# Descending rows of pairs, nodes' ends beside later pairs, and half-size checks in a four-layer graph kernel

## The chip, the cores and the metric

The kernel runs on one core of one Trainium2 chip. The time is the device time of one execution in microseconds; lower is better. Engines are called PE (TensorE), DVE (VectorE), ACT (ScalarE), POOL (GpSimd) and SP (SyncE, which issues most DMAs). PEld is PE's loading of weights.

## The reference

Four graph layers over 4096 nodes of 64 features with one dense 0/1 adjacency of 4096 x 4096. Each layer is fed the normalised, rectified x and added to it:

```python
h = relu(layernorm(x)); x = x + L0(h, adj)   # multi-head graph attention
h = relu(layernorm(x)); x = x + L1(h, adj)   # hyperbolic attention over pairs
h = relu(layernorm(x)); x = x + L2(h, adj)   # neighbours' mean
h = relu(layernorm(x)); x = x + L3(h, adj)   # last 100 neighbours, decayed by rank
```

The layers in question are the last three, cut to what is computed:

```python
# L1
att = sigmoid(left[:, None] + right[None, :] + b) * adj
support = einsum('ij,ijd->id', att, logmap(x[:, None], x[None], c))  # log of a distance
out = proj(expmap(x, support, c), c)      # norms, a tanh, roots: per node
# L2
deg = clip(adj.sum(1) + 1, 1); z = concat([X, (adj @ X + X) / deg], 1) @ W + b
out = relu(z) / max(norm(relu(z)), 1e-12)
# L3
rank = cumsum(adj != 0, 1); deg = rank[:, -1:]; k = minimum(deg, 100)
w = (adj != 0) * where(rank - (deg - k) > 0, 0.5 ** (deg - rank), 0)
out = w @ (X @ weight) + bias
```

## The kernel before, in words

There are 128 partitions, 32 blocks of 128 nodes, 8 groups of 4 blocks (512 nodes) and 4 quarters of 8 blocks. The time up to 1190 us of the span is layer 0 and preparation, which the change leaves alone.

**Layer 1, pairs** (`pairs_fast`, L2253). The 8 x 8 pairs of groups are symmetric in distance, so the list of jobs (L2270) holds 36: rows gi ascending from 0, and in each the columns gj from 0 to gi. A job reads two edge tiles nm (one on the diagonal), makes scores with PE and a sigmoid on ACT (`score_pair`, L2290), a distance with PE, a sigmoid and a Square on ACT (`distance` L2312, `square` L2327), multiplies on DVE (`factor` L2334, `weigh` L2341), transposes the factor on PE and multiplies again for the other direction (`turn`, L2348: the transposes L2353, the multiply L2356), and sums in fp32 on PE (`sums` and `last_column` through `add_up`, L2363). Sums over gj go to the bank acci, kept through a row; sums over gi to accj, which `bring` (L2403) adds into VT (128 x 4096) after each job. The diagonal job ends a row, and its acci is copied to VT first.

**The written order.** Inside `in_order()` every instruction of DVE, ACT and PE is chained to the one written before it on its engine. The pairs' loop (L2422) is a software pipeline with four slots s = 0 to 3 for each job: in one turn it finishes job n - 1, sums job n, weighs n + 1 and measures n + 2. POOL and SP are not chained. Outside `in_order()` a scheduler orders the instructions by readiness and by their place in the program.

**Checks.** The fast layers need an adjacency of zeros and ones. `check_rows` (L958, its instruction L960) reads raw tiles of the adjacency on DVE and adds up what is not 0 or 1 into a column of `bad`. There are 64 tiles of 128 x 2048 (1 MB, loaded by SP, two buffers); the pairs' loop takes most of them, one or two a job, and layer 3 takes the rest by halves of 128 x 1024 (32 instructions) in 2 of 3 iterations from the 16th on (L2936).

**Layer 1, nodes' ends** (`finish_steps` L2452, then `norm_steps` L972, then `nodes` L2602). A generator for each quarter: 8 transposing matmuls pvt out of VT (L2471), the multiply that leaves PSUM (L2475), about 40 DVE operations of 128 x 512 or 128 x 8, Square on ACT (L2491), two roots and a tanh on ACT (L2500, L2520, L2503), the layernorm with its own Square and root (L985, L991), and the split of h in two half-precision parts HH (L2605, L2608, L2612). HH lies in the memory of XA_all, which the distances of the pairs read (XC, XH). A generator yields after each step, True where the next waits for another engine. After all pairs, and in a written order, a loop (L2615 on) runs the four quarters one after the other, with up to 7 steps of the next one put into the waits (two at a wait).

**Layer 2.** The degree and neighbour sums of nodes 0 to 2047 come first: HH against all edges, 8 steps of q ascending, four banks nacc (L2754) and one dc (L2764), from a PSUM pool of six banks (L2744). Then `layer2_group` (L2674) runs for pairs of groups (`in_turn`, L2731, alternates two generators): pz (L2680, L2683), norm, residual, layernorm, transposes tr (L1008), psup (L2717), the split into SS. Nodes 2048 to 4095 come as four `segment`s (L2792: nacc L2802, dc L2811), which also fill a plate of edge counts, plate1 (L2824), from which `rank_rows` (L2739) makes the ranks that layer 3 adds to. There are four pairs of groups in all, called 1 to 4.

**Layer 3** (loop L2924, in a written order). 64 iterations: `ranks` (pv: L2860, L2868), `clamp` (L2877, on ACT L2882 and DVE L2884), `add_up` (sacc, L2892), `bring` (L2906) for the output. Its PSUM pools ps_sacc (2 banks) and ps_v (4 banks), L2846, are opened after layer 2's six have been closed; the pool `misc` of two banks serves both.

Of the kernel before, what the change touches and what calls it, by code (L numbers as in the profile page):

```python
# [25 lines left out]
P = 128  # L26
# [29 lines left out]
F_C = 1186.920286584489  # L56

HW = N // 2
NS = HW // G
HB = NB // 2  # L60
# [776 lines left out]
def kernel(  # L837
# [76 lines left out]
    bad = npool.tile([P, 2 * NB + 2 + NB // 2], F32, name="bad")  # L914
# [37 lines left out]
    def load_rows(pool, c):  # L952

        raw = pool.tile([P, HW], F32, name="raw", tag="raw", bufs=2)
        nc.sync.dma_start(raw, adjT[c % NB * P : (c % NB + 1) * P, c // NB * HW : (c // NB + 1) * HW])
        return raw

    def check_rows(raw, at):  # L958

        nc.vector.scalar_tensor_tensor(  # L960
            raw, raw, 0.0, raw, ALU.is_gt, ALU.not_equal, accum_out=bad[:, at : at + 1]
        )

    def count_odd(pool, c):
        check_rows(load_rows(pool, c), c)

    todo = iter(range(2 * NB))
# [4 lines left out]
    def norm_steps(bs, wide, tag, act=True):  # L972
# [18 lines left out]
        nc.scalar.activation(var, var, AF.Sqrt, bias=eps_t, scale=1.0 / D)  # L991
        yield True
        nc.vector.reciprocal(var, var)
# [55 lines left out]
    with ExitStack() as l0:  # L1049
# [259 lines left out]
        with ExitStack() as pa:  # L1309
# [49 lines left out]
            with in_order():  # L1359
# [87 lines left out]
                nc.vector.tensor_reduce(bad[:, 2 * NB : 2 * NB + 1], tn[:, 0:HS], AX.X, ALU.max)  # L1447
# [488 lines left out]
        with ExitStack() as ob:  # L1936
# [47 lines left out]
            with in_order():  # L1984
# [79 lines left out]
                nc.vector.tensor_scalar(bad[:, 2 * NB + 1 : 2 * NB + 2], sp, SPREAD, None, ALU.is_gt)  # L2064
# [188 lines left out]
    def pairs_fast(es, VT):  # L2253
# [16 lines left out]
        jobs = [(gi, gj) for gi in range(NG) for gj in range(gi + 1)]  # L2270
        edges, sig, far, accs, squares = {}, {}, {}, {}, {}

        with ExitStack() as ss:
# [129 lines left out]
            def bring(gi, gj):  # L2403
                if gi == gj:
                    acci = accs.pop(gi)
                    nc.vector.tensor_copy(VT[0:D, grp(gi)], acci[D : 2 * D])
                    nc.vector.tensor_copy(VT[D : 2 * D, grp(gi)], acci[0:D])
                nc.vector.tensor_tensor(VT[:, grp(gj)], VT[:, grp(gj)], accs.pop("j"), ALU.add)
                del far[gi, gj]
                for way in ways(gi, gj):  # L2410
                    del sig[way], edges[way]

            def check_edges():
                c = next(todo, None)
                if c is not None:
                    count_odd(work, c)
# [5 lines left out]
            with in_order():  # L2422
                for n in range(-2, len(jobs) + 1):
# [3 lines left out]
                    for s in range(4):  # L2427
# [11 lines left out]
                        if later:  # L2439
                            distance(*later, s)  # L2440
                            if s % 2:
                                square(*later, s - 1)
                        if s == 1 and soon:
                            factor(*soon)
                        if n >= 0 and (s == 2 or s == 0 and (not now or now[0] == now[1])):
                            check_edges()
                        if s == 3 and soon:
                            weigh(*soon)
                            for _ in range(2 if n < 0 else 0):
                                check_edges()  # L2450

    def finish_steps(bs, VQ, VT, fold_v, pabs, f, f2, kp, pf, ac2, wide, ps):  # L2452
# [14 lines left out]
        for g in range(bs.start // GB, bs.stop // GB):  # L2467
            pt = ps.tile([P, GB, D1], F32, name="pvt", tag="misc")
# [31 lines left out]
        nc.scalar.activation(un, un, AF.Sqrt)  # L2500
        yield True
        nc.vector.tensor_tensor(arg, un, kp[:, bs], ALU.mult)
        nc.scalar.activation(arg, arg, AF.Tanh)  # L2503
        nc.vector.reciprocal(un, un)
# [7 lines left out]
        nc.vector.tensor_scalar(one2, xu, p2c, 1.0, ALU.mult, ALU.add)  # L2512
        nc.vector.tensor_tensor(den, ac2[:, bs], uu, ALU.mult)
# [6 lines left out]
        nc.scalar.activation(pp, pp, AF.Sqrt)  # L2520
# [5 lines left out]
        nc.vector.reciprocal(pp, pp)  # L2526
# [12 lines left out]
        yield from norm_steps(bs, wide, "fat")  # L2539
# [5 lines left out]
    def layers_fast(es, wide, *sums):  # L2545
        HO2 = N // 4
        NK = HO2 // G
        cp = es.enter_context(tc.tile_pool(name="lconst", bufs=1))
# [21 lines left out]
        for i, unit in enumerate((1.0 / VALH, 1.0 / (LO * VALH))):  # L2570
# [11 lines left out]
        HH, SS = (  # L2582
            t.rearrange("p (b s d) -> p b s d", s=2, d=D)
            for t in (XA_all.bitcast(F16)[:, 0:N], XA_all.bitcast(F16)[:, N:])
        )
# [10 lines left out]
        ready = []  # L2596

        QB = NB // 4  # L2600

        def nodes(bs):  # L2602
            yield from finish_steps(bs, *sums, wide, ps)
            hs = wide.tile([P, QB, D], F32, name="hs", tag="fat")
            nc.scalar.activation(HH[:, bs, 0, :], h[:, bs], AF.Copy, scale=VALH)  # L2605
            yield True
            ready.append(
                nc.vector.scalar_tensor_tensor(  # L2608
                    hs, h[:, bs], VALH, HH[:, bs, 0, :], ALU.mult, ALU.subtract
                )  # L2610
            )
            nc.scalar.activation(HH[:, bs, 1, :], hs, AF.Copy, scale=LO)  # L2612


        quarters = [nodes(slice(b, b + QB)) for b in range(0, NB, QB)]  # L2615
        with in_order():
            for quarter, after in zip(quarters, quarters[1:] + [iter(())]):
                most = 7
                for wait in quarter:
                    for _ in range(min(2, most) if wait else 0):  # L2620
# [41 lines left out]

# [380 lines left out]
```

## Time and profile before

| what | us |
|---|---|
| median of 3 runs (lowest, highest) | 1974.12 (1970.68, 1974.84) |
| the profiled execution's own time | 1974.73 |
| its span on the core | 1973.0 |
| mean granted PE clock | 0.943 |
| busy PE / PEld / DVE | 1773.5 / 827.7 / 1596.4 |
| busy ACT / POOL | 1424.0 / 89.3 |
| pairs of layer 1, from and to | 1190 to 1644 |
| the four writes of HH (a quarter each) | 1675.95, 1692.97, 1710.0, 1726.93 |
| first pz of the four pairs of groups | 1743.3, 1759.9, 1779.5, 1808.2 |
| first pv of layer 3; PE's last work | 1812.4; 1965 |

The times of a profile come from one execution. In its rows L is the line of the kernel; a group shows what it writes, an arrow and what it reads, by the names of the program (the names are those of the first tile in a memory: `XAf` stands for HH, `who` for the value that L2475 makes, `LDf` for blk). "x" is the number of instructions. Brackets at the end give the idle time before and what ended it. Start times are from the start of the span. A busy PE is not PE at its peak, and PEclk is the clock that it was granted as a share of the full one.

### The profile page before, as it was taken

What the parts mean: (1) busy time and instruction counts of PE and PEld (TensorE: products, weight loads), DVE (VectorE), ACT (ScalarE), POOL (GpSimd) and SP (SyncE); (2) the same over time, 40 slices, a digit from 0 to 9 for tenths busy, and PEclk for the clock granted to TensorE, in tenths of its full rate; (3) what the DMA queues carried; (4) which work ended last, traced back from release to release, by engine and by line L of the source; (5) the groups of instructions that cost most, each with busy time, mean ns of one, the idle gap of its engine ahead of it and who ended that gap; (6) DMA issues with size and microseconds to landing.
All of it is one profiled execution on the core that took longest, in us unless ns stands there. A gap on an engine that the chain in (4) does not pass through costs nothing. (4 is left out here: it accounts for less than half of the span.)

```text
span 1973.0 us, 44405 instructions
## 1 busy us (share of the span) xinstructions
PE 1773.5 (90%) x19367; PEld 827.7 (42%) x19367; DVE 1596.4 (81%) x2378; ACT 1424.0 (72%) x1461; POOL 89.3 (5%) x127
## 2 busy tenths in 40 slices
PE   5889999999999989998599968999999994899998
PEld 3444444454444445444244442233333332355433
DVE  5769998998779988997768867888887878755676
ACT  2769888899778887995579956777777772333565
POOL 2000100100000000000111100000000001000000
PEclk8889999999999999998699976999999996898999
DMA  8946665325211111102255515543443435342584
GB/s 112 178 127 103 103 102 71 143 107 199 114 50 50 50 50 55 56 2 76 87 182 182 191 34 193 171 144 118 150 144 122 139 103 194 129 128 88 165 276 158
DMA packets 136698, 239.06 MB, mean 121 GB/s; under 512 B 15607, under 2 KB 104999, under 8 KB 122759
## 3 DMA queue, kind: packets, MB, share of 16 engines
q1 hardware_dynamic: 121964, 194.00, 29.4%
q0 software_dynamic: 14528, 42.13, 12.3%
q8 instruction: 153, 2.51, 0.5%
q14 instruction: 53, 0.43, 0.1%
HBM read 245.37 MB, written 49.46 MB: 149 GB/s over the span
## 5 line engine op out<-in xcount | busy, mean ns | idle before, releaser
L1213 ACT ACTIVATE st<-srow,nt 128x2048 int8<-128x2048 f32 x352 | 682.9, 1994 | 90.3 <-DVE B L1219 89.0
L1219 DVE TENSOR_TENSOR B<-st,mres 128x1024 int32<-128x1024 int32 x256 | 311.6, 1220 | 65.1 <-PE accC L1549 39.4
L1549 PE MATMUL accB<-B,ybh 128*32 128x512 fp8e4 x3072 | 256.6, 383 | 18.7 <-DVE B L1219 18.5
L1549 PEld LDWEIGHTS <-ybh 128*32 128x32 bf16 (+1 forms) x6656 | 179.1, 97 | 210.9 <-issue 56.4
L1549 PE MATMUL accC<-B,ycn 128*32 128x512 fp8e4 x2272 | 227.8, 380 | 1.2 <-issue 1.2
L1549 PE MATMUL accC<-mres,ych 128*32 128x512 fp8e4 x2272 | 228.1, 381 | 0.0
L1549 PE MATMUL accD<-B,ybh 128*32 128x512 fp8e4 x2048 | 207.6, 384 | 2.1 <-DVE h L1681 2.1
L1207 DVE TENSOR_SCALAR st<-srow,nt 128x2048 uint8<-128x2048 f32 x160 | 205.3, 1284 | 1.8
L2363 PE MATMUL accj<-sg,who 128*64 128x512 f32 (+1 forms) x512 | 196.7, 614 | 6.4 <-DVE sg L2356 5.9
L2363 PE MATMUL acci<-sg,who 128*64 128x512 f32 (+1 forms) x512 | 196.7, 614 | 0.0
L2319 ACT ACTIVATE yt<-pu,consts 128x512 f32<-128x512 f32 x144 | 98.6, 686 | 97.9 <-PE pu L2318 97.8
L2308 ACT ACTIVATE sg<-pl,rb 128x512 f32<-128x512 f32 x256 | 160.7, 678 | 7.8 <-PE pl L2303 4.7
L1549 PEld LDWEIGHTS <-ych 128*32 128x32 f16 x4096 | 117.6, 97 | 115.3 <-issue 10.2
L1549 PE MATMUL accL<-B,ybh 128*32 128x512 fp8e4 x1536 | 158.0, 387 | 3.6 <-DVE h L1680 3.6
L960 DVE SCALAR_TENSOR_TENSOR raw<-raw 128x2048 f32<-128x2048 f32 (+1 forms) x80 | 148.4, 1856 | 3.3 <-DMA raw<-in_adj_dram 3.3
L1213 ACT ACTIVATE st<-srowo,nto 128x1024 int8<-128x1024 f32 x128 | 138.1, 1138 | 16.3 <-DVE B L1219 13.9
L1227 DVE TENSOR_TENSOR C<-B,mres 128x1024 int32<-128x1024 int32 x114 | 139.5, 1224 | 3.1
L1549 PE MATMUL accC<-C,ych 128*32 128x512 fp8e4 x1824 | 124.0, 383 | 5.3 <-DVE C L1227 5.2
L2882 ACT ACTIVATE w3b<-pv 128x512 int16<-128x512 f32 x160 | 85.3, 596 | 52.9 <-issue 34.3
L2356 DVE SCALAR_TENSOR_TENSOR sg<-pf,sg 128x512 f32<-128x512 f32 x112 | 72.1, 685 | 38.7 <-PE pf L2353 38.7
L2297 PE MATMUL pl<-nm,noid 128*128 128x512 fp8e4 x256 | 82.3, 393 | 13.7 <-ACT sg L2308 13.0
L1549 PEld LDWEIGHTS <-ycn 128*32 128x32 f16 x2272 | 66.1, 98 | 62.1 <-issue 3.2
(515 smaller groups left out, 2738.8 us busy)
## 6 DMA issues: line engine op xcount, KB each, us to landing
raw<-in_adj_dram SPq DMA_DIRECT2D x64, 1024.0 KB, 5.6
mo<-edges SPq DMA_DIRECT2D x32, 512.0 KB, 4.0
noedge<-nmo POOLq DMA_DIRECT2D x32, 512.0 KB, 3.9
nm<-noedge SPq DMA_DIRECT2D x64, 256.0 KB, 3.0
m<-edges SPq DMA_DIRECT2D x32, 512.0 KB, 5.5
srow<-srow_d SPq DMA_DIRECT2D x15, 1024.0 KB, 7.8
mres<-in_adj_dram POOLq DMA_DIRECT2D x8, 1024.0 KB, 36.1
edges<-in_adj_dram POOLq DMA_DIRECT2D x8, 1024.0 KB, 15.0
```

The source lines that it names most:

```text
L960: nc.vector.scalar_tensor_tensor(raw, raw, 0.0, raw, ALU.is_gt, ALU.not_equal, accum_out=bad[:, at : at + 1])
L1207: nc.vector.tensor_scalar(st[:, i, :].bitcast(U8), srow, negs[:, i : i + 1], EDGE, ALU.is_gt, ALU.mult)
L1213: nc.scalar.activation(st[:, i, :], srow, AF.Sign, bias=negs[:, i : i + 1], scale=-1.0)
L1219: nc.vector.tensor_tensor(B.bitcast(I32), st.bitcast(I32), edges.bitcast(I32), ALU.bitwise_and)
L1227: nc.vector.tensor_tensor(C.bitcast(I32), B.bitcast(I32), edges.bitcast(I32), ALU.bitwise_xor)
L1549: ins = nc.tensor.matmul(acc[k * O : (k + 1) * O, :], lhsT=values, rhs=moving(k), start=start, stop=stop,)
L2297: nc.tensor.matmul(pl, lhsT=noid, rhs=nm[:, b, :].bitcast(F8), start=True, stop=False)
L2308: nc.scalar.activation(sg[:, b0 + k, :], pl, AF.Sigmoid, bias=rb[:, j : j + 1], scale=1.0)
L2319: nc.scalar.activation(far[gi, gj][:, b, :], pu, AF.Sigmoid, bias=nb_t, scale=2.0 * DIST_K / (DIST_S * DIST_S),)
L2356: nc.vector.scalar_tensor_tensor(v[:, t, :], pf, F_K3, v[:, t, :], ALU.add, ALU.mult)
L2363: nc.tensor.matmul(acc[r : r + n, :], lhsT=XQ[:, src, cols], rhs=w, start=start, stop=stop)
L2882: nc.scalar.activation(wk, pvs[i, k], AF.Relu)
```

## The change

1. Jobs go by descending rows, (7, 0) first and (0, 0) last. Row 7 copies accj into VT, all later ones add; the diagonal's halves of acci are added.
2. After the diagonal of rows 6, 4 and 2, the quarter made of groups gi and gi + 1 is complete, and the part of XA under its HH is no longer read. Its `nodes` generator then runs in the pairs' loop, one step a slot (two at s = 2; the first two, which use a bank of ps_f for pvt, only at odd s). The quarter of row 2 is held before its first root. After the pairs the rest of it and the quarter of groups 0 and 1 run as before, with up to 12 steps, three at a wait.
3. In steps beside pairs the three roots are an estimate made on DVE from the bits of the number and three Newton steps on POOL (12 instructions).
4. Checks are 128 halves of 128 x 1024 (512 KB) with four loads asked ahead. In the order that was built, 60 stand in the pairs (none while a quarter's end is under way), 28 from there to the end of layer 2 (7 of them among the last ends of quarters) and 40 in layer 3's last 40 iterations.
5. Layers 2 and 3 share ps_sacc (2 banks) and ps_v (4). Layer 2's first sums take the edges by descending q, and the transposes of h descend too. plate1 and its rank_rows stand in iteration 16 of layer 3.

```diff
-        jobs = [(gi, gj) for gi in range(NG) for gj in range(gi + 1)]
+        jobs = [(gi, gj) for gi in reversed(range(NG)) for gj in range(gi + 1)]
+        ends, held, beside = [], [], [True]
...
             def bring(gi, gj):
+                accj = accs.pop("j")
+                if gi == NG - 1:
+                    nc.vector.tensor_copy(VT[:, grp(gj)], accj)
+                else:
+                    nc.vector.tensor_tensor(VT[:, grp(gj)], VT[:, grp(gj)], accj, ALU.add)
                 if gi == gj:
                     acci = accs.pop(gi)
-                    nc.vector.tensor_copy(VT[0:D, grp(gi)], acci[D : 2 * D])
-                    nc.vector.tensor_copy(VT[D : 2 * D, grp(gi)], acci[0:D])
-                nc.vector.tensor_tensor(VT[:, grp(gj)], VT[:, grp(gj)], accs.pop("j"), ALU.add)
+                    for to, r in ((0, D), (D, 0)):
+                        half = VT[to : to + D, grp(gi)]
+                        nc.vector.tensor_tensor(half, half, acci[r : r + D], ALU.add)
+                    if gi % 2 == 0 and gi:
+                        bank = lambda: ps_f.tile([P, G], F32, name="pf", tag="pf")
+                        ends.append([nodes(gi * GB, bank, beside), 0, *(["last"] if gi == 2 else [])])
...
+            def check_edges(n):
+                for _ in range(n):
+                    if len(todo) + len(ahead) > CHECKS_2 + CHECKS_3:
+                        check_rows(work, CHECKS_2 + CHECKS_3)
+
+            def end_nodes(s):
+                most = 1 + (s == 2)
+                while ends and most:
+                    if s % 2 == 0 and ends[0][1] < 2:
+                        return
+                    wait = next(ends[0][0], None)
+                    ends[0][1] += 1
+                    if wait is None:
+                        ends.pop(0)
+                    elif wait == ROOTS and ends[0][2:]:
+                        held.append(ends.pop(0)[0])
+                    most = 0 if wait else most - 1
...
+                        busy = bool(ends)
+                        if now:
+                            end_nodes(s)
                         if s == 1 and soon:
                             factor(*soon)
-                        if n >= 0 and (s == 2 or s == 0 and (not now or now[0] == now[1])):
-                            check_edges()
+                        if n >= 0 and later and not busy and s % 2 == 0:
+                            check_edges(2 if s or now[0] == now[1] else 1)
                         if s == 3 and soon:
                             weigh(*soon)
-                            for _ in range(2 if n < 0 else 0):
-                                check_edges()
+                            check_edges(4 if n < 0 else 0)
...
+    def inverse_root(name, v, pool):
+        y, t = (pool.tile([P, v.shape[1]], F32, name=n, tag=n) for n in (name, name + "t"))
+        nc.vector.tensor_scalar(
+            y.bitcast(I32), v.bitcast(I32), -0.5, ROOT_BITS, ALU.mult, ALU.add
+        )
+        for _ in range(3):
+            nc.gpsimd.tensor_tensor(t, y, y, ALU.mult)
+            nc.gpsimd.tensor_tensor(t, t, v, ALU.mult)
+            nc.gpsimd.tensor_scalar(t, t, -0.5, 1.5, ALU.mult, ALU.add)
+            nc.gpsimd.tensor_tensor(y, y, t, ALU.mult)
+        return y
...
+        raw = pool.tile([P, CW], F32, name="raw", tag="raw", bufs=4)
+        nc.sync.dma_start(raw, adjT[c // 4 * P : (c // 4 + 1) * P, c % 4 * CW : (c % 4 + 1) * CW])
...
+        if beside[0]:
+            yield ROOTS
+        if beside[0]:
+            norm, un = un, inverse_root("un_root", un, wide)
+            nc.gpsimd.tensor_tensor(norm, norm, un, ALU.mult)
+            nc.gpsimd.tensor_tensor(arg, norm, kp[:, bs], ALU.mult)
+            yield True
+            yield True
+            nc.scalar.activation(arg, arg, AF.Tanh)
+        else:
+            nc.scalar.activation(un, un, AF.Sqrt)
...
-                most = 7
+                most = 12
                 for wait in quarter:
-                    for _ in range(min(2, most) if wait else 0):
+                    for _ in range(min(3, most) if wait else 0):
...
         def in_turn(one, other):
-            for _ in zip_longest(one, other):
-                pass
+            for n, _ in enumerate(zip_longest(one, other)):
+                if n and len(todo) + len(ahead) > CHECKS_3:
+                    with tc.issue_after(valued[-1].ins) if valued else ExitStack():
+                        check_rows(work, CHECKS_3)
...
-        with tc.tile_pool(name="ps_nacc", bufs=6, space=PSUM) as ps_acc:
-            accs = [ps_acc.tile([P, G], F32, name="nacc", tag="nacc") for _ in range(NS)]
-            dc = ps_acc.tile([P, G], F32, name="dc", tag="nacc")
+        ps_acc = es.enter_context(tc.tile_pool(name="ps_sacc", bufs=2, space=PSUM))
+        ps_v = es.enter_context(tc.tile_pool(name="ps_v", bufs=4, space=PSUM))
...
+        accs = [rank_bank("nacc") for _ in range(NS)]
+        dc = sum_bank("dc")
+        for n, q in enumerate(reversed(range(NQ))):
...
+        def segment(k):
+            acc, dc = sum_bank("nacc"), rank_bank("dc")
...
-                checks = u and (n - PAIRS) % 3
+                checks = n >= 4 * PAIRS - CHECKS_3
                 w = clamp(pvs, checks)
                 if checks:
...
+                    check_rows(work)
+                if n == PAIRS:
+                    later_ranks()
```

## The prediction

> **What bounds the kernel now.** I read the page's table of engines first (PE 90% of the span), then cut the part that the change touches into stages with the table of windows, whose columns are us, busy time of PE, PE's weight loads, DVE, ACT and POOL, then PE's clock, DMA share and GB/s.
>
> ```profile
> 1188.00:1645.00 457.00, 433.70 (x2288) 147.95 (x2288) 371.89 (x421) 335.48 (x473) 0.62 (x3) 0.96 0.43 144
> 1645.00:1676.00 31.00, 7.32 (x32) 6.98 (x32) 27.98 (x76) 8.16 (x14) 8.44 (x14) 0.54 0.64 237
> 1676.00:1722.00 46.00, 38.12 (x240) 17.13 (x240) 34.95 (x117) 15.41 (x25) 1.61 (x1) 0.79 0.35 119
> ...
> 1745.00:1812.00 67.00, 62.68 (x434) 40.57 (x433) 33.78 (x100) 19.99 (x52) 7.02 (x10) 0.90 0.40 117
> 1812.00:1966.00 154.00, 150.41 (x860) 62.24 (x859) 113.25 (x202) 92.81 (x180) 1.82 (x3) 1.00 0.58 195
> 1411.00:1424.00 13.00, 13.00 (x74) 4.67 (x72) 10.12 (x12) 10.03 (x15) 0.00 (x0) 1.00 0.37 123
> ```
>
> The rows are the pairs; the nodes' ends alone and beside the first half of layer 2's sums; layer 2's groups; layer 3; and one off-diagonal pair. PE is full in the pair (13.00 of 13) with DVE and ACT at 10. After the pairs DVE is busy 28 of 31 us while PE has 7: a serial stretch. What PE waits for there:
>
> ```profile
> 1676.00 0.61 PE L2754 MATMUL nacc<-m,XAf 128*128 128x512 fp8e4 x1 [15.07 <-ACT XAf L2612]
> 1693.03 7.08 PE L2754 MATMUL nacc<-m,XAf 128*128 128x512 fp8e4 x32 [0.16 <-ACT XAf L2612]
> 1710.05 9.76 PE L2754 MATMUL nacc<-m,XAf 128*128 128x512 fp8e4 x32 [3.53 <-ACT XAf L2612]
> ```
>
> Each quarter of HH (the XAf that L2612 writes) starts 32 sums. The fourth is written at 1726.9, so a quarter costs 17 us, some 15.5 of it DVE work. Milestones: last pair sum 1644.2, last HH 1726.9, first pz 1743.3, fourth pair of groups 1808.2, layer 3's first pv 1812.4, end 1973.0.
>
> **The change, part by part.** *Order of rows.* The same 36 jobs run, an off-diagonal one taking 12.85 us, a diagonal one 10.7 to 12.3. Short rows, where ACT and DVE bind, go to the end, and the checks that stand between the last sum and the adds go away: -2 (bounds -9 and +4, as no descending row is in the trace).
>
> *Three quarters' ends into the pairs.* Can DVE hold them? One pair on DVE's timeline (start, length):
>
> ```profile
> 1415.05 0.69 DVE L2408 TENSOR_TENSOR VT<-VT,accj 128x512 f32<-128x512 f32 x1 [1.13 <-PE accj L2363]
> 1415.69 1.29 DVE L2356 SCALAR_TENSOR_TENSOR sg<-pf,sg 128x512 f32<-128x512 f32 x2
> 1416.89 2.35 DVE L2337 SCALAR_TENSOR_TENSOR yt<-sqy,yt 128x1024 f32<-128x1024 f32 x2
> 1421.00 1.29 DVE L2356 SCALAR_TENSOR_TENSOR sg<-pf,sg 128x512 f32<-128x512 f32 x2 [1.75 <-PE pf L2353]
> 1422.20 2.28 DVE L960 SCALAR_TENSOR_TENSOR raw<-raw 128x2048 f32<-128x2048 f32 x1
> 1424.41 0.08 DVE L960 DVE_READ_ACCUMULATOR raw<-raw 128x1 f32 x1
> 1424.41 2.36 DVE L2344 SCALAR_TENSOR_TENSOR sg<-yt,sg 128x1024 f32<-128x1024 f32 x2
> ```
>
> Without the check the pair keeps 7.8 us of DVE. A quarter's 16.2 us of steps spread over about 6 jobs is 2.7 a job: 10.5 of 12.85, hidden. The other jobs get three half checks of 1.29 (1.21 at 128x1024 in layer 3, plus 0.08 for the read): 11.7 of 12.85, also under PE. If PE's cover were gone, the ends would cost their 3 x 16 = 48. The built order confirms that the steps stand beside pairs, at one step a slot of 3.2 us.
>
> PE is not free there: each quarter brings 8 pvt matmuls, 1.8 us at full clock, into jobs that PE fills: 3 x 1.8 = +5.4.
>
> DVE, ACT and PE keep a written order, so a step that waits holds all behind it. The multiply of L2475 waits for its pvt (behind two turns on PE), with factor, weigh and then the turns' multiplies queued behind it, for which PE's sums wait: 1 to 1.5 a quarter. ACT's Square and Tanh stand ahead of the sigmoids that free PE's pl and pu banks: 0.2 to 0.6 each. The root is now a seed on DVE and 12 small POOL instructions (up to 14 with their products). The nearest POOL row is a 0.19 us copy of 16 columns; the trace has no 8-column arithmetic there, so I take 0.25, a chain of 3 to 3.5 us, against two slots (6.4 us) before DVE or ACT reads it. Its lower bound is nothing. POOL's list holds nothing else beside the pairs.
>
> Here a rule of the Trainium skill speaks against the change. On DVE's timeline of layer 2:
>
> ```profile
> 1769.98 0.17 DVE L993 RECIPROCAL ln_var<-ln_var 128x4 f32<-128x4 f32 x1
> 1770.19 0.97 DVE L994 SCALAR_TENSOR_TENSOR h<-h,ln_var 128x256 f32<-128x256 f32 x1
> ```
>
> and on POOL's timeline:
>
> ```profile
> 1770.14 0.73 POOL L2725 TENSOR_TENSOR x<-x,b3f 128x256 f32<-128x256 f32 x1 [0.59 <-DVE ln_var L993]
> ```
>
> L994 takes 0.42 elsewhere; beside the POOL add it ends only after that. "SBUF — State Buffer", section "Who interferes with whom", says that a VectorE instruction with two SBUF inputs and a GpSimd instruction that reads SBUF exclude each other for a whole instruction, whoever comes first. The row shows DVE as the victim: 36 POOL instructions a quarter cost DVE at most 0.25 each, 9 us spread over slack. By the rule POOL can be the victim too: each of 14 could sit behind one 1.2 us factor or weigh, 14 x 1.2 = 17 against 6.4 of cover. These are 4.7 of DVE's 12.85 us, with gaps between, so I side with the row: a few stalls. All waits of this paragraph: +8 (bounds 0 and +50, the latter as a rival). Last pair sum: 1644.2 - 2 + 5.4 + 8 = 1655.6.
>
> *From the last pair sum to the last HH: 82.7 before.* What stays is the adds into VT (2.6), the rest of the quarter held at its first root (10.5 of DVE), the last quarter (15.5) and waits (5), as ACT still answers and reloads tables at 1.28 each. The built order also puts 7 half checks here, 7 x 1.29 = 9. Sum 42.6, so -40. Half of layer 2's sums can now start before this; they were already hidden but for the last 32.
>
> *Last HH to the first pz: 16.4 before.* Order of sums reversed, four banks of ps_v: the last quarter's 32 nacc and dc still follow, plus sharing: +2.3 (bounds 0 and +5).
>
> *Layer 2's groups.* Checks enter as 0, 7, 7, 7 in the four pairs of groups, 9 us of DVE each. PE binds here, 62.7 of 67, with DVE at half. In pairs 2 and 3 the later segments' 64 matmuls cover the longer chain: +1. The fourth has behind it only layer 3's start. In before, four of its iterations of 2.16 us filled PE until 1826.8; with shared banks and the new order about 1.5 fit: 9 - 1.5 x 2.16 + 3 of lost overlap, +9 (bounds +3 and +14). The fourth chain is late next where the nodes' wait goes.
>
> *Layer 3.* Each of the last 40 iterations now has a half check.
>
> ```profile
> 1864.00:1877.00 13.00, 13.00 (x74) 4.80 (x72) 9.94 (x17) 8.47 (x16) 0.00 (x0) 1.00 0.93 321
> 1877.00:1890.00 13.00, 13.00 (x74) 4.81 (x72) 9.94 (x17) 8.47 (x16) 0.00 (x0) 1.00 0.71 243
> ```
>
> Six iterations of 2.16 hold four checks. With six, DVE does one clamp of 0.69 and 1.29: 1.98 of 2.16, just under PE. An iteration needs 0.52 MB of raw and 0.26 of edges, 365 GB/s against at most 321 seen; four raw tiles and two of edges ahead (4 MB) lend the difference of 44 GB/s x 86 us = 3.8 MB. Raw's loads wait in SP for a check to free their tile, with edges queued behind, for which PE waits. The later ranks add five matmuls and three DVE copies. Together +2.5 (bounds 0 and +9).
>
> Sum: +11.4 - 40 + 2.3 + 1 + 9 + 2.5 = -13.8. The profiled execution took 1974.73 with a span of 1973.0, so 1961 by it; the median of the runs is 0.6 lower: 1960.4. A measurement of this kernel can tell 0.2% (4 us) from no change, so "same" is 1970.2 to 1978.1.
>
> **Rivals.** *Better cover.* The waits beside the pairs cost 0, layer 2's last chain only 4 and the two ends 4 less: 8 + 5 + 4 less, about 1943. For it: pairs leave DVE and ACT 2 us or more each; against it: the orders are written out, and each pvt multiply has to wait.
>
> *Freed time taken by layers 2 and 3.* DVE's checks or SP's raw loads hold the m blocks (5.5 us to land), or the shared banks keep layer 3 from starting: +10 to +14 on the sum, 1970 to 1975, about nothing. For it: four checks' worth of work left the pairs for stages where chains set the time; against it: PE's cover in pairs 2 and 3.
>
> *Slower: POOL's roots are starved by VectorE.* Six chains (un, pp and ln of the two whole quarters; the third is held at its first root) stand beside pairs, each with a reader on DVE or ACT that waits in order. If each takes 14 to 15 us of the rule's 17 against 6.4 of cover, each stalls PE 8: 48 less the few waits counted, +42, about 2003. It turns the gain into a loss at 13.8/6 = 2.3 us a chain beyond the sum, a chain of some 10 us, 0.7 us for each POOL instruction. For it: the rule; against it: the gaps of 1 to 2 us in DVE's rows of the pair.
>
> **How the numbers follow.** The sum 0.45 (1950 to 1969, at 1960); better cover 0.20; time taken by layers 2 and 3 0.19 (six parts in ten of it within 0.2%); roots starved, or a like stall of the pairs, 0.16. Faster: 0.45 + 0.20 + 0.04 = 0.69. Same: 0.12, some of it from milder starving. Slower: 0.19. The range 1938 to 1985 leaves a tenth on each side.
>
> **What would show it.** Right: pair jobs near 12.9 us while ends run, the last sum near 1656; four HH writes, two of them before it; 43 us from there to the last; DVE full in the fourth pair of groups, with PE waiting for its tr. Wrong: long idle of ACT or DVE released by POOL's roots; jobs of 14 us or more beside ends; PE waiting for m or edges from DMA; or a fall in PE's clock beside the pairs, which the sum does not contain.

## The result, and the profile after

The changed kernel takes 1968.1 us (median of 20 runs, 1958.4 to 1974.2) where the kernel before takes 1972.1 in the same comparison (20 runs). The ratio is 0.9978, with a 95% interval of 0.9966 to 0.9989: 4.3 us faster, between 2.2 and 6.7. It is faster, as forecast, but by 4 us where the steps gave 14. The profiled execution took 1970.55 us with a span of 1968.8.

The milestones of the two profiles, taken from PE's timeline and from ACT's writes of HH, with what the prediction's steps gave:

| stage | before | after | difference | forecast |
|---|---|---|---|---|
| to the last pair sum | 1644.2 | 1657.0 | +12.8 | +11.4 |
| from there to the last HH | 82.7 | 44.2 | -38.5 | -40 |
| last HH to the first pz | 16.4 | 19.7 | +3.3 | +2.3 |
| first pz to the fourth | 64.9 | 71.4 | +6.5 | +1 |
| fourth pz to the end | 164.8 | 176.5 | +11.7 | +11.5 |
| span | 1973.0 | 1968.8 | -4.2 | -13.8 |

In one profile each of the first four stages comes out 1 to 6 us worse than forecast. The same stages in the table of windows of the changed kernel (us, busy time of PE, PE's weight loads, DVE, ACT, POOL, then PE's clock, DMA share and GB/s):

```profile
1188.00:1657.00 469.00, 440.71 (x2320) 153.07 (x2320) 371.42 (x545) 343.27 (x487) 28.68 (x81) 0.95 0.33 104
1657.00:1701.00 44.00, 33.45 (x204) 15.11 (x205) 37.55 (x103) 9.74 (x17) 10.36 (x14) 0.81 0.72 261
1701.00:1720.90 19.90, 19.88 (x131) 10.01 (x129) 8.94 (x22) 5.69 (x12) 0.61 (x1) 1.00 0.90 297
1720.90:1792.30 71.40, 67.11 (x447) 42.48 (x446) 46.84 (x126) 20.22 (x52) 7.04 (x10) 0.86 0.72 216
1792.30:1819.00 26.70, 18.44 (x81) 11.77 (x80) 18.28 (x47) 8.37 (x21) 1.45 (x2) 0.61 0.49 156
1819.00:1962.00 143.00, 141.48 (x808) 57.09 (x806) 108.91 (x181) 88.75 (x168) 0.38 (x1) 1.00 0.69 234
```

The second row is what the change is for: PE is now busy in 33 of 44 us where it had long waits. The fifth is new: after the fourth pz PE has 18.4 of 26.7 us, at a clock of 0.61, and DVE 18.3. By DVE's timeline the 28 checks that left the pairs run in the second, fourth and fifth row: 7, 16 and 5.

PE's timeline shows the two longest waits that the change brought. The first line stands in the last short rows, the last one in front of a pv of layer 3, which waits for a clamp (w3b) on DVE; the line between them is what is left of the wait for HH:

```profile
1650.38 1.97 PE L2394 MATMUL accj<-sg,who 128*64 128x512 f32 x2 [7.10 <-DVE VT L2439]
1692.82 9.26 PE L2822 MATMUL nacc<-m,XAf 128*128 128x512 fp8e4 x32 [6.87 <-ACT XAf L3061]
1808.40 0.58 PE L2927 MATMUL pv<-late_x,LDf 32*128 32x512 bf16 x1 [7.07 <-DVE w3b L2951]
```

What DVE does during the last of these waits, on its timeline of the fourth pair of groups: the steps of two groups with checks (L973) between them, and the clamp that PE waits for comes behind all of it.

```profile
1799.25 0.42 DVE L2749 TENSOR_TENSOR zt<-pz,deg 128x256 f32<-128x256 f32 x1 [1.52 <-PE pz L2740]
1799.59 1.22 DVE L973 SCALAR_TENSOR_TENSOR raw<-raw 128x1024 f32<-128x1024 f32 x1
...
1801.82 1.22 DVE L973 SCALAR_TENSOR_TENSOR raw<-raw 128x1024 f32<-128x1024 f32 x1
...
1803.49 1.20 DVE L973 SCALAR_TENSOR_TENSOR raw<-raw 128x1024 f32<-128x1024 f32 x1
...
1805.14 1.19 DVE L973 SCALAR_TENSOR_TENSOR raw<-raw 128x1024 f32<-128x1024 f32 x1
...
1807.66 0.68 DVE L2951 TENSOR_SCALAR w3b<-pv 128x512 int16<-128x512 f32 x1
```

### The profile page after: what moved, and what is told of

Its sections match the earlier page's. It is cut to its first block, busy times and chain, and to the rows that moved or that the text cites. A ratio compares the mean times of both kernels' runs of the same rounds, so it can differ in the third digit from the quotient of the medians.

```text
span 1968.8 us, 44691 instructions
## 1 busy us (share of the span) xinstructions
PE 1783.0 (91%) x19367; PEld 829.7 (42%) x19367; DVE 1595.8 (81%) x2464; ACT 1421.0 (72%) x1459; POOL 117.8 (6%) x205
## 3 DMA queue, kind: packets, MB, share of 16 engines
q0 software_dynamic: 14528, 42.13, 12.4%
## 4 chain that ended last, share of the span: by engine, by line
PE 55%; DVE 21%; ACT 14%; issue 6%; DMA 4%; SPq 0%; DVEq 0%; POOL 0%; ACTq 0%; POOLq 0%
ACT st L1243 9%; PE accj L2394 9%; DVE B L1249 7%; PE accC L1579 7%; PE accB L1579 3%; PE pv L2935 3%; PE acco L2186 3%; PE pf L2384 3%; PE sacc L2959 3%; DVE st L1237 3%; PE pl L2328 2%; PE accD L1579 2%; PE pu L2348 2%; PE pl L2334 2%; PE accL L1579 2%
## 5 line engine op out<-in xcount | busy, mean ns | idle before, releaser
L1579 PEld LDWEIGHTS <-ybh 128*32 128x32 bf16 (+1 forms) x6656 | 179.1, 97 | 211.4 <-issue 56.5
L1579 PEld LDWEIGHTS <-ych 128*32 128x32 f16 x4096 | 118.7, 98 | 117.1 <-issue 12.5
L973 DVE SCALAR_TENSOR_TENSOR raw<-raw 128x1024 f32<-128x1024 f32 x128 | 153.9, 1216 | 0.3 <-DMA raw<-in_adj_dram 0.3
L2368 DVE SCALAR_TENSOR_TENSOR yt<-sqy,yt 128x1024 f32<-128x1024 f32 x72 | 84.8, 1218 | 3.4 <-ACT sqy L2360 3.4
```

The costliest lines, as they stand in the source:

```text
L973: nc.vector.scalar_tensor_tensor(raw, raw, 0.0, raw, ALU.is_gt, ALU.not_equal, accum_out=bad[:, c : c + 1])
L1579: ins = nc.tensor.matmul(acc[k * O : (k + 1) * O, :], lhsT=values, rhs=moving(k), start=start, stop=stop,)
L2368: nc.vector.scalar_tensor_tensor(y, squares.pop((gi, gj, b0)), F_K1, y, ALU.add, ALU.mult)
```

## The experiments

Each run was timed beside the kernel before on the same chip. I give its median, and the difference from the kernel before: the ratio less one, times 1973 us, with the interval in brackets. On this scale the changed kernel is at -4.3 [-6.7, -2.2]. Two runs of programs that differ in nothing that matters (e10 and e17 below) came out 4 us apart, so differences under 4 us between two such runs say little.

**The checks behind the pairs.** e1 leaves out all 28, e2 the last seven, e3 the seven among the ends:

```diff
-CHECKS_2 = 28
-    todo = list(range(4 * NB))
+CHECKS_2 = 0     # e2, e3: 21
+    todo = [c for c in range(4 * NB) if not 60 <= c < 88]   # e2: 81..87, e3: 60..66
+    nc.vector.memset(bad[:, 60:88], 0.0)
...
+                if valued and n and ...   # e3 alone: none ahead of the first psup
```

> The changed kernel with the 28 half checks between the pairs and layer 3 left out altogether (their loads too); 60 checks in the pairs and 40 in layer 3 stay. Theory A (these checks stretch DVE's serial chains in the nodes' ends and in layer 2, PE runs out of work and its clock is then granted at half): the last HH comes 8 us earlier, the stage from the first pz to the end of PE's work falls from 241 to about 224, the half-clock spell at 1789 to 1813 of the changed kernel is gone: 20 to 25 us less than the changed kernel, about 1946. Theory B (the shared PSUM banks, the order of the segments' sums and the later ranks cost it): at most the 8 us of the nodes' ends, 1958 to 1962, with the half-clock spells still there.

1946.9 us, -28.0 [-32.2, -23.7]: 24 less than the changed kernel. First theory confirmed; the rival's 1958 to 1962 is out. From the first pz to the end of PE's work its profile has 223 us, the changed kernel's 241.

> The changed kernel with only the last 7 half checks of layer 2, those in the fourth pair of groups, left out. Theory A: the idle of 7 us of PE before layer 3's clamps and the half clock behind it go, 10 to 15 us less than the changed kernel, about 1955. Theory B: 3 us or less, since a wait for banks of ps_v takes the place of the wait for DVE.

1954.7 us, -20.5 [-24.3, -16.8]: 16 less than the changed kernel, from seven checks of 1.29 us. The idle of 7 us is gone from its trace; the longest wait for a clamp there is 1.2.

> The changed kernel with only the 7 half checks left out that stand among the last quarters' ends; 7 stay in each of the pairs of groups 2, 3 and 4. Theory A: the last HH 8 to 9 us earlier, PE's wait of 6.9 us for it shorter, 6 to 8 us less in all, about 1961. Theory B says the same here; if the time is equal, PE's remaining first half of layer 2 sums were the bound instead of the chain.

1966.9 us, -5.9 [-9.3, -2.6]: 2 less instead of 6 to 8. In its profile the last HH came 36.4 us behind the last pair sum instead of 44.2, which is 7.8 less, but the first pz only 4.8 earlier (PE's own sums became the limit), and the rest was lost behind it. The expectation missed.

**Order, ends, layer 3.** e4 is the kernel before with the rows turned round; e7 undoes the placing of the ends, and with it the roots on POOL; e8 leaves out layer 3's 40 checks.

```diff
-        jobs = [(gi, gj) for gi in range(NG) for gj in range(gi + 1)]            # e4, and its bring
+        jobs = [(gi, gj) for gi in reversed(range(NG)) for gj in range(gi + 1)]
...
-                        ends.append([nodes(gi * GB, bank, beside), 0, ...])       # e7
+        for b0 in (24, 16, 8, 0):
+            ends.append(nodes(b0, lambda: ps.tile([P, G], F32, name="pvt", tag="misc"), [False]))
...
-CHECKS_3 = 40                                                                     # e8
+CHECKS_3 = 0
```

> The kernel before with only the order of rows turned round (descending, with the adds into VT that this needs); checks, ends and layers as before. By the prediction -2 us (between -9 and +4) against the kernel before. If the tail of short rows costs more than the checks hide (the single bank of accj makes each short job wait for the add of the job ahead), it is 3 to 8 slower.

1972.2 us, +0.8 [-1.4, +3.0]: no gain from the order.

> The changed kernel with only the placing of the nodes' ends undone: all four quarters' ends follow the pairs, with ACT's roots; descending rows, checks and layers 2 and 3 as in the changed kernel. By the prediction's terms the ends beside the pairs take 40 us off the stage behind the pairs and cost 5.4 + 8 in the pairs: this one about 27 us slower than the changed kernel, 1995. If the gain of the ends was small from the start (PE's clock, or a chain that only moved), less than 15, below 1983.

1991.1 us, +16.2 [12.4, 20.1]: 20.5 slower than the changed kernel. This is what the ends beside the pairs are worth, less than the 27. Its stages (windows: the pairs, then to the last HH):

```profile
1188.00:1640.30 452.30, 433.63 (x2297) 149.50 (x2297) 341.16 (x442) 335.73 (x473) 0.66 (x3) 0.97 0.34 108
1640.30:1720.80 80.50, 43.20 (x248) 21.15 (x247) 68.28 (x205) 25.33 (x41) 11.42 (x14) 0.70 0.50 171
```

Against the first two rows of the changed kernel: the pairs cost 16.7 us more with the ends beside them (7.1 of it PE's busy time, 9.6 idle), and the stage behind them is 36.3 shorter (80.5 to 44.2).

> The changed kernel with the 40 half checks of layer 3 left out (with their loads), the other 88 as they are. By the prediction's term for layer 3, 2.5 us less than the changed kernel, about 1965.5; none at all if DVE's 1.98 of 2.16 us and the loads ahead hide them fully. If the loads or the clamps behind the checks bind PE, 8 or more less, below 1960.

1969.2 us, -3.7 [-5.9, -1.4]: no difference from the changed kernel. Layer 3 hides its 40 checks whole; in the changed kernel's iterations with a check and the loads at 353 GB/s PE is busy 13.00 of 13:

```profile
1890.00:1903.00 13.00, 13.00 (x81) 5.79 (x81) 10.54 (x19) 8.18 (x16) 0.00 (x0) 1.00 1.02 353
```

**All checks done, elsewhere.** e5, e9 and e10 change only CHECKS_2 and CHECKS_3 (14 and 54; 7 and 57; 0 and 64). e6 puts 88 into the pairs:

```diff
-                        if n >= 0 and later and not busy and s % 2 == 0:
-                            check_edges(2 if s or now[0] == now[1] else 1)
+                        if n >= 0 and s % 2 == 0 and (s or not busy):
+                            check_edges(1 if busy else 2 if s or now and now[0] == now[1] else 1)
```

> The changed kernel with all checks, but 14 of layer 2's 28 moved on to layer 3, whose last 54 iterations now hold one each; none is left in the third (but 4 at its start) and fourth pairs of groups. Theory A (checks in layer 2's late chains and the half clock behind them): 13 to 18 us less than the changed kernel, 1950 to 1955. Rival (layer 3 has no room: 0.52 MB of raw and 0.26 of edges in each iteration ask for 363 GB/s where 321 were seen, and DVE is at 1.98 of 2.16 us): PE waits for edges or for DVE's clamps, 5 to 10 us come back, 1958 to 1963.

1955.8 us, -16.2 [-20.1, -12.2]: 12 less than the changed kernel, at the edge of the first theory's 1955.

> The changed kernel with all checks, but layer 2's 28 moved forward into the pairs: one in each job beside a quarter's end, and the rest in diagonal jobs and the last short row. Theory A: layer 2 runs as in the run without its checks; the jobs beside ends rise to 11.8 us of DVE of 12.85 and hide it, the last short rows cost 5 or so: about 1950 to 1953. Rival (DVE's written order has no slack beside the ends, each check there delays a multiply for which PE waits): 14 x 1.3 = 18 us more, 1965 to 1970.

1963.7 us, -9.9 [-13.2, -6.3]: 6 less, between the two. The pairs end only 4.0 us later in its profile (1661.0), so the jobs beside ends do hide a check; but the eight in the last short row delay the first sums of layer 2 (1673.6, in the changed kernel 1662.5), and the last HH to the first pz takes 28.3 us where the changed kernel has 19.7.

> The changed kernel with all checks: 64 in the pairs (four more in a diagonal job that is free), 7 among the last quarters' ends, none in layer 2's groups, 57 in layer 3. Theory A (the checks in the groups of layer 2 are the cost, layer 3 has room): within 3 us of the run that leaves layer 2's checks out, plus 1 for the nodes' ends: 1946 to 1950. Rival (layer 3's loads, 363 GB/s over 57 iterations, run dry): as the run with 54 or slower, 1955 to 1962.

1956.4 us, -19.5 [-22.9, -16.2]: the first theory's 1946 to 1950 missed. The number is the rival's, but not its reason, since the next run loads more in layer 3 and is faster.

> As the run with 57 in layer 3, with the 7 checks of the nodes' ends moved to layer 3 too: one in every one of its 64 iterations, none between the pairs and layer 3. Theory A: 1944 to 1949. Rival (loads): 64 x 0.52 and 64 x 0.26 MB in 138 us are 364 GB/s with only the four tiles asked ahead; at 330 GB/s that takes 152 us, less the 2 MB ahead: 8 us more than the run with 57.

1950.6 us, -23.7 [-27.2, -20.3]: 19 less than the changed kernel with all the work done, and just above the first theory's 1949. The rival's dry loads don't come: layer 3 from 1805 on runs at 301 GB/s and 0.87 of the DMA engines with PE at 137.4 of 140:

```profile
1716.00:1777.20 61.20, 57.12 (x444) 35.85 (x443) 30.24 (x94) 19.84 (x52) 7.08 (x10) 1.00 0.39 115
...
1805.00:1945.00 140.00, 137.37 (x769) 54.56 (x768) 114.32 (x192) 94.09 (x180) 0.38 (x1) 1.00 0.87 301
```

The first row is its stage from the first to the fourth pz: 444 matmuls, where the changed kernel has 447, in 61 us instead of 71, at a clock of 1.00 instead of 0.86. The ten are PE's busy time, 57.1 for 67.1; its idle is 4 us in both.

Not every place in layer 3 is free, though. PE's sums of an early iteration start 2.62 us apart in e10, and 2.16 in e16 (below), which has no check in its first 24 iterations:

```profile
1811.51 1.03 PE L2959 MATMUL sacc<-w3b,XAf 128*128 128x512 bf16 x4
1814.12 1.03 PE L2959 MATMUL sacc<-w3b,XAf 128*128 128x512 bf16 x4
...
1804.31 1.03 PE L2959 MATMUL sacc<-w3b,XAf 128*128 128x512 bf16 x4
1806.47 1.03 PE L2959 MATMUL sacc<-w3b,XAf 128*128 128x512 bf16 x4
```

The first two rows are e10's, the others e16's. The first 20 iterations take 56.5 us in e10 and 52.0 in e16; later both have 2.16. In e9, whose checks start with the eighth iteration, they are 2.62 us apart up to the sixteenth and 2.16 behind it. So a check has a price in the first 16 iterations, about the 4 us by which e10 stays behind e1. What holds PE there was not tested.

**Is it the clock?** e11 adds 12 matmuls to fill the idle of PE, after the step that takes the norm's root in `layer2_group`:

```diff
+            for _ in range(6 if b0 >= HB + 2 * GB else 0):
+                nc.tensor.matmul(pz.rearrange("p b d -> p (b d)"), lhsT=HH[:, 0]..., rhs=HH[:, 0:4]..., start=True, stop=True)
```

> The changed kernel with 12 matmuls of 128 x 512 more, whose results are not used (each of the last two groups of layer 2 writes its own bank again after it was read), placed on PE between the fourth pz and layer 3's clamps, where PE idles 7 us. They take 2.6 us at full clock, 5.1 at half. If the half clock behind that idle has a price of its own: the spell at 1789 to 1813 ends earlier, and the time is 2 to 4 us less although PE has more to do. If only DVE's chain counts: no change, or 1 to 3 us more.

1970.7 us, -3.7 [-5.7, -1.8]: as the changed kernel. The spell of half clock ended 8 us earlier in its profile (1805, with one more of 3.4 us behind it) and the time stayed, since the clamp behind DVE's chain came no sooner after the fourth pz, 16.1 us in both:

```profile
1799.69 5.30 PE L2760 MATMUL pz<-XAf 128*128 128x512 f16 x12
1806.83 0.37 PE L2929 MATMUL pv<-late_x,LDf 32*128 32x512 bf16 x1 [1.84 <-DVE w3b L2953]
```

The half clock behind the last idle has no price of its own that this run can tell; DVE's chain sets the time there. The spell before the fourth pz, where PE does not wait, is not tested by it.

**DVE's time or the loads?** Leaving out the checks takes away both. e13 keeps the loads, e14 keeps DVE's instructions.

```diff
+            raw[:, :8], raw[:, :8], 0.0, raw[:, :8], ALU.is_gt, ...    # e13: in the 28
...
+    todo = [c for c in range(4 * NB) if not 60 <= c < 88]               # e14
+        spare = VT[:, 0:CW]
+                        nc.vector.scalar_tensor_tensor(spare, spare, 0.0, spare, ALU.is_gt, ALU.not_equal, accum_out=VT[...])
```

> The changed kernel with the 28 checks between the pairs and layer 3 cut to 8 of their 1024 columns: the loads of 512 KB and the waits for them stay, DVE's 1.2 us each goes. If DVE's time in the groups' chains is the cost: as the run without these checks, 1945 to 1950. If the loads are (they share the queue and HBM with the edges of layer 2 and of layer 3's first iterations): little less than the changed kernel, 1962 to 1968.

1952.8 us, -19.5 [-23.7, -15.4]: 15 of e1's 24 are back with the loads in place. What makes the other 9 stays open.

> The changed kernel with these 28 checks made on a part of VT that is no longer needed, so that DVE's instructions stay (7 among the nodes' ends, 7 in each of the groups' pairs 2 to 4, spread over their steps by the order of DVE's work) and their 14.7 MB of loads go. If DVE's time is the cost: as the changed kernel, 1964 to 1970. If the loads are: as the run without these checks, 1945 to 1950.

1975.3 us, +4.1 [2.0, 6.1]: 8 slower than the changed kernel, though 14.7 MB of loads are gone. DVE's time is most of the cost. Here the checks also sit inside the steps of each group, since the edit holds them there, and PE waits 7.1 us for the last transposes.

**Where in the groups?** e12 leaves out the 14 checks of pairs 2 and 3 and holds the last seven in pair 4's steps. e15 only holds them, e16 only leaves out.

```diff
+    todo = [c for c in range(4 * NB) if not 67 <= c < 81]      # e12, e16; CHECKS_2 = 14
+                if len(turns) in (1, 4) and n and ...           # e12, e16
...
+            (valued.append if b0 >= HB + 2 * GB else id)(nc.vector.tensor_reduce(nrm, sq, AX.X, ALU.add))   # e12, e15
```

> The changed kernel with only the 14 half checks in the second and third pairs of groups left out; 7 stay among the nodes' ends and 7 in the fourth pair (held in its steps by the order of its own DVE work, so that they don't gather ahead of it). By the prediction's step (the segments' matmuls cover the longer chain in pairs 2 and 3, 1 us) within 2 us of the changed kernel, 1966 to 1969. By the difference of the other runs (21 for all 28, 13 for the last 7, 1 for the nodes' 7) 7 less, about 1961, with the stage from the second pz to the fourth at 46 to 50 us where the changed kernel takes 56, and PE's half clock in it shorter.

1966.9 us, -5.9 [-8.3, -3.6]: 2 less. As the prediction's step had it, the checks of pairs 2 and 3 cost little while pair 4 keeps its own. In the profile the second pz to the fourth did shrink to 48 us from 56, but 4 of the 8 came back behind it.

> The changed kernel with all 28 checks, and only the seven of the fourth pair of groups held in that pair's steps, as in the run without those of pairs 2 and 3. If holding them there is what ate that run's gain: 4 to 7 us slower than the changed kernel, 1972 to 1975. If the terms really do not add up: no change, 1966 to 1970.

1969.3 us, -3.6 [-5.7, -1.2]: holding them changes nothing, since the changed kernel has them there anyway.

> The run without the 14 checks of pairs 2 and 3 once more, with the last seven not held: the order then has all seven ahead of the fourth pair's first DVE work, where PE still sums segments. If holding them ate the gain: 7 us or more less than the changed kernel, 1955 to 1961. If the checks of pairs 2 and 3 cost nothing while pair 4 keeps its own: 1966 to 1969.

1956.1 us, -18.0 [-21.9, -13.8]: 12 less than e12, with the same checks done. (Its profile is of the fastest of its six executions, 1941.2 us, in which PE lost no clock from the first pz on.) The order has the seven in one block ahead of the fourth pair's first step, and there PE still has segments to sum. DVE's timeline, then PE's:

```profile
1764.27 1.21 DVE L973 SCALAR_TENSOR_TENSOR raw<-raw 128x1024 f32<-128x1024 f32 x1
...
1772.90 1.22 DVE L973 SCALAR_TENSOR_TENSOR raw<-raw 128x1024 f32<-128x1024 f32 x1
```

```profile
1764.02 6.20 PE L2868 MATMUL nacc<-m,XAf 128*128 128x512 fp8e4 x28
...
1784.18 0.37 PE L2927 MATMUL pv<-late_x,LDf 32*128 32x512 bf16 x1 [1.44 <-DVE w3b L2951]
```

So the same seven instructions cost about 12 us more between the fourth pz and its transposes than 10 us earlier. That they cost nothing there isn't shown: e16 is 10 us behind e1, which lacks the seven among the ends too.

**What the ends lose.** Both runs start from e10.

```diff
-        nc.gpsimd.memset(hT2[D : D + 1, :], 1.0)
+        with not_before_nodes(): nc.gpsimd.memset(hT2[D : D + 1, :], 1.0)     # e17
...
-                    elif wait == ROOTS and ends[0][2:]:
+                    elif ends[0][1] == 2 and ends[0][2:]:                      # e18
```

> The run with 64 checks in layer 3 and, beside it, POOL's memset of 1 x 4096 (one row of hT2) held until the last nodes' end. In the changed kernel a DVE instruction of 128 x 8 that takes 0.17 elsewhere takes 3.27 beside this memset, in the chain of the last two quarters. If that lock is a term of the lost gain: 2 to 4 us less than without the move, about 1947.5. If PE's first half of layer 2's sums is the bound there anyway: no change, 1949 to 1952.

1953.6 us, -19.9 [-24.9, -14.8], which says nothing of the memset: in its trace it still begins at 1664.2, inside the ends, so the edit did not move it. It serves as a second measurement of e10. What the memset costs is open.

> The run with 64 checks in layer 3 and, beside it, the quarter of row 2 held after its two first steps instead of before its first root, so that none of its steps stands in rows 1 and 0. In the changed kernel PE idles 7.1 us there for the add into VT, which stands on DVE behind these steps. If this idle is the price of the last quarter's steps: the last pair sum about 6 us earlier, and 4.5 us of DVE more behind it: 0 to 3 us less, 1947 to 1951. If the idle comes from the short rows alone: 4 us more, about 1955.

1949.4 us, -25.3 [-31.0, -19.5]: the fastest complete version, though not told apart from e10. In its profile the pairs end 7.5 us earlier (1647.4, in e10 1654.9), and the idle of 7.1 is down to

```profile
1641.67 1.85 PE L2394 MATMUL accj<-sg,who 128*64 128x512 f32 x2 [2.20 <-DVE VT L2439]
```

so most of that idle was made by the last quarter's steps, not by the short rows. In e7, with no ends in the pairs, it is 0.8.

## Why the prediction was wrong, by its own steps

The mechanism was right: the ends came off the serial stretch, and the moved checks took much of it back. The sizes were not. Summing the prediction's steps for e7 (everything but the ends' place) gives -2 for the order, +2 behind the pairs (82.7, less three whole checks of 2.3, plus 9), +2.3, +1, +9 and +2.5: +14.8. Measured: +16.2. So that part holds as a sum, though by luck: the checks and the order cost some 5 and 3 more than forecast (below), the stage behind the pairs and layer 3 some 4 and 2.5 less. **The step that failed is the ends beside the pairs**: the same sums give -13.8 - 14.8 = -28.6 for it, and the runs -20.5. The second mis-sized term is the checks of the fourth pair of groups, 9 forecast and 16 measured (e2). By the profiles of e7 and of the change:

- *In the pairs*, 5.4 for pvt and 8 for waits: measured 7.1 of PE's busy time (at a clock of 0.95 instead of 0.97) and 9.6 of idle, 16.7 in all. The waits were not spread as I had them, 1 to 1.5 in each quarter. Most stood in one place, a wait of 7.1 us in rows 1 and 0 where e7 has 0.8, where the last quarter's multiplies, reduces and its Square's result stand on DVE ahead of weigh and of the add into VT, and PE had no other job to do. e18, where that wait is 2.2, shows it.
- *Behind the pairs*, 42.6 us were forecast and 44.2 measured. But I had taken before's 17 us a quarter as the price of what goes away, and the new loop, with up to 12 steps put into the waits instead of 7, already does four quarters in 80.5 (e7) instead of the 84.8 of the sum: 36 came off, not 42. A part of that gain needs no pairs; that the loop's 12 steps make it was not tested alone.

**What the sum lacks is PE's clock behind the first pz.** In the table of stages the largest miss is layer 2's groups, +6.5 for +1. The same stage and the one behind it (to PE's last work), twice before and then twice after:

```profile
1743.30:1808.20 64.90, 60.58 (x419) 38.81 (x417) 30.95 (x94) 19.99 (x52) 7.02 (x10) 0.89 0.38 110
1808.20:1965.00 156.80, 154.21 (x890) 65.70 (x890) 115.66 (x206) 92.81 (x180) 1.82 (x3) 1.00 0.59 198
...
1720.90:1792.30 71.40, 67.11 (x447) 42.48 (x446) 46.84 (x126) 20.22 (x52) 7.04 (x10) 0.86 0.72 216
1792.30:1961.60 169.30, 159.88 (x887) 68.86 (x885) 126.88 (x225) 97.11 (x188) 1.83 (x3) 0.94 0.66 222
```

In the groups PE idles 4.3 us in both kernels, so DVE's longer chains made no new wait there. Its busy time grew by 6.5: 3 of it is clock (10.0 us lost, as one less the clock, for 6.8), the rest goes with 28 more matmuls, since layer 3's first pv (1779.8) now come before the fourth pz. Over both stages the time grew by 19, for 12.5 forecast: 7 more of waits, and 9.5 more of clock lost while PE was busy, for which the sum has no term (by e11 the half clock behind the last idle costs nothing of its own, so not all of this is time). The last row of the table of stages, 11.7 for 11.5, is luck too: pair 4's checks cost more than forecast, layer 3's nothing.

The other points:

- *The 28 checks*: 9 + 1 + 9 = 19 forecast, 24 measured (e1). The sum was nearly right, the places were not. The seven among the ends: 9 forecast, 2 measured (e3), because PE's sums are next behind that chain. Pairs 2 and 3: 1 forecast, 2 measured (e12). In their own stage they do more: from the second pz to the fourth the nine profiles of the changed kernel and its variants that keep DVE's checks there have 52 to 60 us, the nine others 45 to 51. Pair 4: 9 forecast, 16 measured (e2), the term that was furthest off. I had let 1.5 iterations of layer 3 cover DVE's 9 us; but layer 3's clamps are on DVE too, behind the checks, so the cover fails with the chain it should cover.
- The terms do not add: 16 + 2 + 2 is not 24, and after e2 the others are worth 8. While pair 4 is late, what is saved ahead of it is waited away there.
- *Order*: -2 forecast, +0.8 [-1.4, +3.0] measured. *Layer 3*: +2.5 forecast, none measured for the last 40 iterations (e8): 1.98 of 2.16 us is enough there, and the loads had room for 64 checks (e10), not only for 40.
- *The rival of layers 2 and 3 taking the freed time* was nearest, with 1970 to 1975; its mechanism (m blocks held by loads, shared banks) is not what the runs show: e13, with all loads kept, is 15 faster. The reason that it gave, work that left the pairs for stages where chains set the time, is. *Better cover* was too hopeful. *Starved roots* did not come: a chain takes 5.1 to 5.6 us, not 3.5, inside the 6.4 of cover. POOL's timeline of the first one, then DVE's row beside it:

```profile
1426.16 1.03 POOL L989 TENSOR_TENSOR un_roott<-un_root 128x8 f32<-128x8 f32 x1 [235.60 <-DVE un_root L985]
1427.28 1.06 POOL L990 TENSOR_TENSOR un_roott<-un_roott,un 128x8 f32<-128x8 f32 x1
1428.43 0.20 POOL L991 TENSOR_SCALAR un_roott<-un_roott 128x8 f32<-128x8 f32 x1
...
1431.55 0.20 POOL L2562 TENSOR_TENSOR arg<-un,kp 128x8 f32<-128x8 f32 x1
...
1425.92 2.35 DVE L2368 SCALAR_TENSOR_TENSOR yt<-sqy,yt 128x1024 f32<-128x1024 f32 x2
```

Two of its 14 instructions take 1.0 instead of 0.20, beside DVE's two factor multiplies, which have two inputs in SBUF; the other five chains too have two such. So POOL can be the loser, as the Trainium skill, "SBUF — State Buffer", section "Who interferes with whom", says of two-input DVE instructions, but twice in a chain, not 14 times.

## What to carry to other kernels

Filler work of one engine is free only where the engine that sets the end has work which does not wait for the same list: ask of each place what is queued behind the filler on its own engine. Seven instructions of 1.3 us cost 12 us more between a chain's first and last step than ahead of its first. Forty cost nothing that could be measured in iterations that PE fills, but the early iterations of the same loop went from 2.16 to 2.62 us. To size a move, measure the moved-from place as the new code would leave it, not as the old code has it.

## What was not expected of the hardware

- A DVE instruction of 128 x 8 took 3.27 us, and the one behind it 3.19, instead of 0.17, beside POOL's memset of one row of 4096 (3.50 us). It is one instance; the three end within 0.03 us of each other. DVE's timeline, then POOL's:

```profile
1667.92 3.27 DVE L2584 TENSOR_SCALAR mden<-mden 128x8 f32<-128x8 f32 x1
1668.00 3.19 DVE L2585 SCALAR_TENSOR_TENSOR pp<-xu,a 128x8 f32<-128x8 f32 x1
...
1667.66 3.50 POOL L2721 MEMSET hT<- 1x4096 f32 x1
```

- PE was granted half its clock for 13 to 14 us while it was fully busy, behind idles of only 0.4 to 1 us. In the changed kernel, by windows of 2 us (busy time, clock, DMA share, GB/s):

```profile
1754.00:1756.00 2.00, 2.00 (x15) 1.00 1.18 290
...
1758.00:1760.00 2.00, 2.00 (x13) 0.68 0.78 197
1760.00:1762.00 2.00, 2.00 (x11) 0.50 0.39 86
...
1772.00:1774.00 2.00, 2.00 (x10) 0.91 0.66 219
```

The Trainium skill, "TensorE: Matmul & The Clock Gate", section "Part 1: The HAM clock gate", has the clock fall after an idle window of about 3.4 us; no such idle stands ahead of this spell, and the measurement decides. Summed as one less the clock, times the time, from the first pz on, the kernels with checks inside pair 4's chain lose 17 to 26 us of clock in their profiles (the change 20, 16 of it while PE was busy), the others 0 to 15 (e10 7, e16 none). The executions of one kernel spread along with it: 1958.4 us at a mean clock of 0.950 and 1974.2 at 0.941, of the same program. That the checks cause the spells is an association; e11 shows only that one of them is without price.
